# A local-attention kernel on one Trainium2 core: AV with V as the stationary operand, and the softmax divided ahead of the transposes

## The chip, the core and the metric

The kernel runs on one core of a Trainium2 chip (trn2). A core has five engines that run side by side: TensorE (PE in the profile; its weight loads are a row of their own, PEld), VectorE (DVE), ScalarE (ACT), GpSimd (POOL) and SyncE (SP), which here only issues DMAs. The metric is the device time of one execution in microseconds (us); lower is better. A "record" below is one line of the hardware trace: a matmul of fp32 data leaves two pairs of records, each a weight load (the stationary operand) and a matmul (the moving operand streamed through it), and an fp32 transpose leaves one pair.

## The reference

The model is a linear recurrence (8 sequences of 512 steps, width 128) and then six layers of local attention and feed-forward on its output. The change touches the attention alone. Cut to that:

```python
DIM = 128; DEPTH = 6; HEADS = 16; DIM_HEAD = 64; WINDOW = 32; QK_SCALE = 8.0
def local_attention(q, k, v):
    b, h, n, d = q.shape                  # 8, 16, 512, 64
    w = WINDOW; nw = n // w
    bq = q.reshape(b, h, nw, w, d)
    ...
    bk2, bv2 = (look(bk), look(bv))       # each block with the one before it: 64 keys
    ...
    sim = jnp.einsum('bhwie,bhwje->bhwij', bq, bk2) * QK_SCALE
    sim = jnp.where(mask, -jnp.finfo(sim.dtype).max, sim)
    attn = jax.nn.softmax(sim, -1)
    out = jnp.einsum('bhwij,bhwje->bhwie', attn, bv2)
    return out.reshape(b, h, n, d)

def attn_layer(x, Wqkv, qs, ksc, Wo):
    ...
    out = local_attention(q, k, v)
    out = out.transpose(0, 2, 1, 3).reshape(b, n, INNER)
    return out @ Wo
```

All of it is fp32.

## The kernel before

**Tiling.** One *group* is one sequence with half of its heads: 8 heads, held as 4 pairs (`GP = 4`). There are 6 layers x 8 sequences x 2 halves = 96 groups (in layer 0, whose input comes out of the recurrence a quarter at a time, a group is a 128-position chunk of four sequences instead; the work is of the same size). A group has 512 positions, worked through in four *slots* of 128 (`t = 0..3`), and a slot has four blocks of 32 queries (`BT = 4`, `QB = 32`), each of which sees 64 keys (`KB = 64`). There are thus 96 x 4 = 384 slots.

**The attention of one slot.** `scores(t)` does 32 small matmuls (4 pairs x 4 blocks x 2 heads of the pair) into a PSUM area `sc` that ScalarE has filled with the mask before (`mask`). `less_max` takes the maximum of each row and subtracts it (two VectorE instructions, from PSUM into the SBUF tile `e`), and `exps` does the exponential on ScalarE in place. One slot later, `turn` transposes the exponentials, four transposes of 128 x 128 into the PSUM tile `tp`, and ScalarE copies them to `eT`. `average` is the product with V, the AV of the title: 32 matmuls, each with 32 columns of `eT` as the stationary operand (64 keys x 32 queries) and 65 columns of V as the moving one, of which the last is a column of ones, so that the sum of the exponentials comes out as a 65th column. The two heads of a pair lie in partitions 0 to 63 and 64 to 127 (`rows`), and the four query blocks go to the four 32-partition strips of the output. The output of each head goes into a PSUM bank of its own (`av`, two of them), queries on the partitions. `divide` (VectorE) inverts the 65th column and multiplies, twice, into `ao`. One slot later again `turn_back` transposes `ao` with four more transposes, so that the head dimension is on the partitions, and ScalarE copies that to `aoT`. `project` multiplies with `Wo` (4 matmuls of 512 columns), once in a group, and `add` adds it to the residual.

**Order.** Nothing reorders the work: the order on every engine is written out by hand in `mixed` and `dense`, which lay one slot's attention of the group `cur` between the projections of the groups behind it in line: `one` (its norms `sums`, its values `values`, its rotary finish) and `two` (`unit_a`, `unit_b`: the query and key projections, 512 columns each), while `old` is the group before (its `project`). `last` is the slot one earlier, `back` the slot two earlier. Each engine works through its own queue in order and waits on semaphores.

**Stages.** While the recurrence still runs (groups up to `NREC = 9`), `mixed` is used: after each piece of TensorE work `rec.tick(us)` issues the next step of the recurrence if at least `PACE = 0.35` us of work have been laid in between. Steps that find no place run `alone`, beside matmuls that only keep TensorE busy (`warm`, L361). After that `dense` is used for the remaining 87 groups, with the feed-forward (`Feed`) laid in after every eight groups.

**Buffers.** The PSUM pool `acc` has two banks, which `tp`, the two `av`, `at` and the feed-forward's output take in turn. `mm` has four banks in the dense stage (three before), and `sc` has two. `e`, `eT` and `ao` have one buffer each, `aoT` one for a whole group. V lies in `vbufs`, 65 wide a head (`VW = DH + 1`), written by `values`, with SBUF-to-SBUF DMAs (`between`) that copy each block next to its neighbour.

Of the kernel before, what the change touches and what calls it, by code (L numbers as in the profile page):

```python
# [27 lines left out]
GP = 4  # L28
# [7 lines left out]
VW = DH + 1  # L36
# [12 lines left out]
def mk_seq_preln_kernel(  # L49
# [44 lines left out]
    for i in range(2):  # L94
        vb = const.tile([P, NBLK, GP, VW], F32, name=f"vbuf{i}")
        nc.gpsimd.memset(vb, 0.0)
        nc.gpsimd.memset(vb[:, :, :, DH:], 1.0)
        vbufs.append(vb)
# [53 lines left out]
    with tc.tile_pool(name="qk", bufs=2) as qkp, tc.tile_pool(  # L152
# [323 lines left out]
        class Group:  # L476
# [172 lines left out]
            def exps(self):  # L649
                nc.scalar.activation(self.e, self.e, AF.Exp, scale=QK_SCALE)  # L650

            def turn(self, t):
                nm = f"{self.nm}_{t}"
                tp = accp.tile([P, GP, P], F32, tag="acc", name=f"tp_{nm}")
                for i in range(GP):
                    nc.tensor.transpose(  # L656
                        tp[:, i, :], self.e[:, i].rearrange("p a k -> p (a k)"), ident
                    )
                rec.tick(0.5)
                self.eT = ep.tile([P, GP, P], F32, tag="eT", name=f"eT_{nm}")  # L660
                nc.scalar.copy(self.eT, tp)  # L661

            def average(self, t):
                self.avs = [
                    accp.tile(
                        [P, GP, P], F32, tag="acc", name=f"av_{self.nm}_{t}_{par}"
                    )
                    for par in range(2)
                ]
                for i in range(GP):  # L670
                    for blk in range(BT):
                        for par, av in enumerate(self.avs):
                            rows = slice(par * KB, (par + 1) * KB)
                            nc.tensor.matmul(  # L674
                                av[blk * QB : (blk + 1) * QB, i, :VW],
                                self.eT[rows, i, blk * QB : (blk + 1) * QB],
                                self.v[rows, BT * t + blk, i, :],
                                start=True,
                                stop=True,
                                skip_group_check=True,  # L680
                            )
                rec.tick(0.8)

            def divide(self, t):
                nm = f"{self.nm}_{t}"
                self.ao[t] = ep.tile(
                    [P, GP, 2, DH], F32, tag="ao", name=f"ao_{nm}", bufs=1
                )
                for par, av in enumerate(self.avs):
                    rc = small.tile([P, GP], F32, tag="rc", name=f"rc_{nm}_{par}")  # L690
                    nc.vector.reciprocal(rc, av[:, :, DH])  # L691
                    nc.vector.tensor_mul(  # L692
                        self.ao[t][:, :, par, :],
                        av[:, :, :DH],
                        rc.unsqueeze(2).to_broadcast([P, GP, DH]),
                    )

            def turn_back(self, t):
                if t == 0:
                    self.aoT = aop.tile([P, GP, S], F32, tag="ao", name=f"aoT_{self.nm}")  # L700
                at = accp.tile([P, GP, P], F32, tag="acc", name=f"at_{self.nm}_{t}")
                for i in range(GP):
                    nc.tensor.transpose(  # L703
                        at[:, i, :], self.ao[t][:, i].rearrange("p a d -> p (a d)"), ident
                    )
                rec.tick(0.5)
                nc.scalar.copy(self.aoT[:, :, t * P : (t + 1) * P], at)  # L707
# [258 lines left out]
        def mixed(n, t, cur, one, two, old, last, lt, back, bt):  # L966
# [10 lines left out]
            if old and t == 1:  # L977
                fill[3] = [lambda: old.project(wo)]
# [22 lines left out]
            if back:  # L1001
                back.turn_back(bt)
# [10 lines left out]
            if one and t == 1:  # L1013
                one.finish(1)
            if last:
# [5 lines left out]
            if last:  # L1021
                last.divide(lt)
# [4 lines left out]
        def dense(t, cur, one, two, old, last, lt, back, bt, feed):  # L1027

            def softmax():
                if cur:  # L1030
                    cur.less_max(t)
                    cur.exps()
                    if t + 1 < NT:
                        cur.mask(t + 1)
                    elif one:
                        one.mask(0)

            if last:
                last.turn(lt)
            if back:  # L1040
                back.turn_back(bt)
# [3 lines left out]
            if cur:  # L1045
                cur.scores(t)
            if t == 0:
                softmax()
# [13 lines left out]
                if last:  # L1062
                    last.average(lt)
                    last.divide(lt)
# [3 lines left out]
            if t == 1:  # L1068
                softmax()
                if old:  # L1070
                    old.project(wo, (0, 1))
                if one:
                    one.finish(1)
                if last:
                    last.average(lt)
                    last.divide(lt)
                if old:
                    old.project(wo, (2, 3))
                    old.add()
                if one:  # L1080
                    one.finish(2)
# [7 lines left out]
            if t >= 2:  # L1089
                if two and not (feed and t == 2):  # L1090
                    two.unit_b(u)
                softmax()
                if last:
# [3 lines left out]
                    last.divide(lt)  # L1097
# [14 lines left out]
        def slot(n, t, feed=None):  # L1112
# [10 lines left out]
            back, bt = (cur, t - 2) if t > 1 else (old, NT - 2 + t)  # L1123
            if n < NREC:
                mixed(n, t, cur, one, two, old, last, lt, back, bt)
            else:
                dense(t, cur, one, two, old, last, lt, back, bt, feed)
# [185 lines left out]
```

## Time and profile before

| What | us |
|---|---|
| Median of 3 runs | 3746.9 (3741.02 to 3747.28) |
| Profiled execution, device time | 3752.48 |
| Its span (first to last instruction) | 3750.3 |
| DVE busy, share of the span | 2585.7 (69%) |
| ACT busy | 1929.7 (51%) |
| POOL busy | 1826.5 (49%) |
| POOL, L548 and L549, the two largest groups of any engine | 766.3 and 756.8 |
| ACT, the copies `eT` (L661) and `aoT` (L707), 320 each | 190.1 and 193.7 |
| DVE, `ao` (L692), 640 | 271.8 |
| `warm` matmuls of the steps that run alone (L361), 182 steps | 69.7 + 49.9 |
| Mean granted TensorE clock | 0.977 of full speed |

The span is read in two parts: up to about 597 us the recurrence runs (512 steps, the last tanh at 596.5 us), and from there on the dense order repeats. The row maxima (L640, one for each slot) show its period: outside the feed-forward, four slots of a group take 28.5 to 31 us, and every eighth group, with a feed-forward between, some 70 us.

### The profile page before, as it was taken

What the parts mean: (1) busy time and instruction counts of PE and PEld (TensorE: products, weight loads), DVE (VectorE), ACT (ScalarE), POOL (GpSimd) and SP (SyncE); (2) the same over time, 40 slices, a digit from 0 to 9 for tenths busy, and PEclk for the clock granted to TensorE, in tenths of its full rate; (3) what the DMA queues carried; (4) which work ended last, traced back from release to release, by engine and by line L of the source; (5) the groups of instructions that cost most, each with busy time, mean ns of one, the idle gap of its engine ahead of it and who ended that gap; (6) DMA issues with size and microseconds to landing.
All of it is one profiled execution on the core that took longest, in us unless ns stands there. A gap on an engine that the chain in (4) does not pass through costs nothing.

```text
span 3750.3 us, 158910 instructions
## 1 busy us (share of the span) xinstructions
PE 3546.2 (95%) x70180; PEld 2137.0 (57%) x70180; DVE 2585.7 (69%) x5200; ACT 1929.7 (51%) x3864; POOL 1826.5 (49%) x780
## 2 busy tenths in 40 slices
PE   8889987999999999999999999999999999999997
PEld 4556664555566556556565565555556565565553
DVE  3455565767677677677677677677677677677673
ACT  2344443545565455455466455455455465465552
POOL 1442332636366366366366366466466465465450
PEclk9988988999999999999999999999999999999998
DMA  4233433554355345345245355355355255355242
GB/s 128 53 93 78 101 84 75 127 117 108 86 117 119 70 113 132 81 105 124 67 114 138 76 115 113 73 130 124 80 115 116 68 130 124 74 115 120 67 111 56
DMA packets 355866, 378.20 MB, mean 101 GB/s; under 512 B 93550, under 2 KB 254572, under 8 KB 355052
## 3 DMA queue, kind: packets, MB, share of 16 engines
q1 hardware_dynamic: 354172, 365.78, 42.7%
q8 instruction: 554, 9.08, 1.1%
q10 hardware_dynamic: 1008, 2.27, 0.2%
q14 instruction: 132, 1.08, 0.1%
HBM read 34.56 MB, written 14.20 MB: 13 GB/s over the span
## 4 chain that ended last, share of the span: by engine, by line
PE 80%; DVE 11%; ACT 4%; issue 3%; DMA 1%; SPq 1%; DVEq 0%; ACTq 0%
PE yo L713 8%; PE rawb L538 8%; PE rawa L526 8%; PE sc L627 8%; PE av L674 5%; PE tp L656 5%; PE nsq L430 4%; PE at L703 4%; PE yf L912 3%; PE xb L281 3%; PE fa L886 3%; PE fg L890 3%; PE vps L587 3%; PE bc L465 2%; PE warm L361 2%
## 5 line engine op out<-in xcount | busy, mean ns | idle before, releaser
L548 POOL TENSOR_TENSOR u<-rope_sb,bs 128x1024 f32<-128x1024 f32 x320 | 766.3, 2395 | 1228.8 <-ACT bs L544 1066.4
L549 POOL TENSOR_TENSOR t<-t,u 128x1024 f32<-128x1024 f32 x320 | 756.8, 2365 | 25.1
L516 DVE SCALAR_TENSOR_TENSOR t<-rawa,par_sb,rope_sb 128x1024 f32<-128x1024 f32 x320 | 410.5, 1283 | 214.9 <-ACT sq L530 200.7
L650 ACT ACTIVATE e<-e 128x512 f32<-128x512 f32 x320 | 201.7, 630 | 371.5 <-DVE e L643 229.6
L565 DVE TENSOR_TENSOR t<-t,bc 128x1024 f32<-128x1024 f32 x320 | 381.9, 1214 | 14.7 <-PE bc L465 10.2
L661 ACT COPY eT<-tp 128x512 f32<-128x512 f32 x320 | 190.1, 594 | 349.1 <-PE tp L656 348.6
L674 PEld LDWEIGHTS av<-vbuf,eT 64*32 64x32 f32 x20480 | 228.0, 105 | 215.0 <-issue 139.1
L526 PE MATMUL rawa<-xbuf,wqk 128*128 128x512 f32 x640 | 342.8, 617 | 0.0
L538 PE MATMUL rawb<-xbuf,wqk 128*128 128x512 f32 x640 | 342.4, 617 | 0.0
L587 PE MATMUL vps<-wv,xbuf 128*64 128x256 f32 x2560 | 315.8, 387 | 8.3 <-DVE xf L864 8.3
L713 PE MATMUL yo<-aoT,wo 128*128 128x512 f32 x640 | 319.5, 622 | 0.9 <-ACT aoT L707 0.9
L627 PEld LDWEIGHTS sc<-kbuf,qT 64*32 64x32 f32 x20480 | 227.2, 105 | 144.8 <-ACT sq L542 57.0
L674 PE MATMUL av<-vbuf,eT 64*32 64x65 f32 x20480 | 283.4, 225 | 6.4 <-issue 5.3
L692 DVE TENSOR_TENSOR ao<-av,rc 128x256 f32<-128x256 f32 x640 | 271.8, 425 | 22.0
L627 PE MATMUL sc<-kbuf,qT 64*32 64x64 f32 x20480 | 282.1, 225 | 1.7 <-issue 1.5
L640 DVE TENSOR_REDUCE mx<-sc 128x8 f32<-128x512 f32 x320 | 219.6, 686 | 91.9 <-PE sc L627 91.7
L281 PEld LDWEIGHTS xb<-hT,s1w 128*128 128x128 f32 x1022 | 168.9, 197 | 172.9 <-ACT hT L289 118.5
L596 ACT COPY vbuf<-vps 128x512 f32<-128x512 f32 x320 | 188.2, 588 | 141.2 <-PE vps L587 138.4
L542 ACT ACTIVATE sq<-rawb 128x512 f32<-128x512 f32 x320 | 189.7, 593 | 129.6 <-PE rawb L538 129.1
L587 PEld LDWEIGHTS vps<-wv,xbuf 128*64 128x64 f32 x2560 | 168.4, 136 | 151.1 <-DVE rc L691 48.5
L289 ACT ACTIVATE hT<-xb 128x8 f32<-128x8 f32 x512 | 91.5, 179 | 291.8 <-PE xb L281 276.5
L643 DVE TENSOR_TENSOR e<-sc,mx 128x512 f32<-128x512 f32 x320 | 221.3, 692 | 11.0
(282 smaller groups left out, 6280.1 us busy)
## 6 DMA issues: line engine op xcount, KB each, us to landing
qT<-t SPq DMA_DIRECT2D x640, 128.0 KB
kbuf<-t SPq DMA_DIRECT2D x640, 128.0 KB
vbuf<-vbuf SPq DMA_DIRECT2D x544, 130.0 KB
vbuf<-vbuf SPq DMA_DIRECT2D x160, 97.5 KB
wqk<-in_w_qkv SPq DMA_DIRECT2D x12, 512.0 KB
xbuf<-xT SPq DMA_DIRECT2D x48, 128.0 KB
xf<-xT SPq DMA_DIRECT2D x24, 256.0 KB
xf<-xT SPq DMA_DIRECT2D x24, 255.5 KB
```

The lines of the kernel that those rows point to most:

```text
L281: nc.tensor.matmul(self.xb[:, k, :], abc[:, 0, :], self.hT[:, (t - 1) % P, :], start=False, stop=True, skip_group_check=True,)
L516: nc.vector.scalar_tensor_tensor(t, self.twice(raw), scale, self.rope(isk, 1), ALU.mult, ALU.mult)
L526: nc.tensor.matmul(raw, self.wqk[:, c, 0], self.xs[:, WINDOW:], start=True, stop=True)
L538: nc.tensor.matmul(raw, self.wqk[:, c, 1], self.xs[:, WINDOW:], start=True, stop=True)
L548: nc.gpsimd.tensor_mul(self.wide(u), self.rope(isk, 0), self.twice(bs))
L549: nc.gpsimd.tensor_add(self.ts[c], self.ts[c], u)
L565: nc.vector.tensor_mul(t, t, self.bcs[c].unsqueeze(1).to_broadcast([P, 2, S]))
L587: nc.tensor.matmul(ps[par * KB : (par + 1) * KB, j], self.xs[:, k0 : k0 + KB], self.wv[:, par * GP * DH : (par + 1) * GP * DH], start=True ...
L627: nc.tensor.matmul(self.sc[blk * QB : (blk + 1) * QB, par, i, :], self.qT[rows, i, q0 : q0 + QB], kT[rows, i, :], start=False, stop=True, ...
L674: nc.tensor.matmul(av[blk * QB : (blk + 1) * QB, i, :VW], self.eT[rows, i, blk * QB : (blk + 1) * QB], self.v[rows, BT * t + blk, i, :], s ...
L692: nc.vector.tensor_mul(self.ao[t][:, :, par, :], av[:, :, :DH], rc.unsqueeze(2).to_broadcast([P, GP, DH]),)
L713: nc.tensor.matmul(self.yp, wo[:, self.g * GP + c, :], self.aoT[:, c, :], start=(c == 0), stop=(c == GP - 1),)
```

## The change

- V becomes the stationary operand of AV (64 keys x 64 head columns) and 32 columns of `eT` the moving one. The output then has the head dimension on the partitions, both heads of a pair in one PSUM bank, and ScalarE copies it straight to `aoT`. `turn_back`, its transposes and the tile `ao` are gone.
- Since the sum over the keys can no longer ride along as a 65th column, the exponentials are summed and divided ahead of `turn`: `exps` now writes a PSUM tile `ex` out of the pool `acc`, and `divide` sums it over the keys, inverts the sums and multiplies into the SBUF tile `p`, which `turn` transposes.
- V is 64 wide (`VW = DH`), and the column of ones is gone with its memset.
- The order: `aoT` is ready a slot earlier (`last` in place of `back`). In `dense`, `scores` now comes first in a slot, `turn` second, and `unit_a` after `less_max`; at `t = 1`, the whole of `project` stands ahead of `average` instead of half of it on each side. In `mixed`, `project` stands between the mask and `average`.

```diff
-VW = DH + 1
+VW = DH
...
-        nc.gpsimd.memset(vb[:, :, :, DH:], 1.0)
...
             def exps(self):
-                nc.scalar.activation(self.e, self.e, AF.Exp, scale=QK_SCALE)
+                self.ex = accp.tile(
+                    [P, GP, 2, KB], F32, tag="acc", name=f"ex_{self.nm}"
+                )
+                nc.scalar.activation(self.ex, self.e, AF.Exp, scale=QK_SCALE)
+
+            def divide(self, t):
+                nm = f"{self.nm}_{t}"
+                rc = small.tile([P, GP, 2], F32, tag="rc", name=f"rc_{nm}")
+                nc.vector.reduce_sum(rc, self.ex, AX.X)
+                nc.vector.reciprocal(rc, rc)
+                self.p = ep.tile([P, GP, 2, KB], F32, tag="p", name=f"p_{nm}")
+                nc.vector.tensor_mul(
+                    self.p, self.ex, rc.unsqueeze(3).to_broadcast([P, GP, 2, KB])
+                )
 
             def turn(self, t):
...
-                        tp[:, i, :], self.e[:, i].rearrange("p a k -> p (a k)"), ident
+                        tp[:, i, :], self.p[:, i].rearrange("p a k -> p (a k)"), ident
...
             def average(self, t):
-                self.avs = [
-                    accp.tile(
-                        [P, GP, P], F32, tag="acc", name=f"av_{self.nm}_{t}_{par}"
-                    )
-                    for par in range(2)
-                ]
+                nm = f"{self.nm}_{t}"
+                if t == 0:
+                    self.aoT = aop.tile([P, GP, S], F32, tag="ao", name=f"aoT_{nm}")
+                av = accp.tile([P, GP, P], F32, tag="acc", name=f"av_{nm}")
                 for i in range(GP):
                     for blk in range(BT):
-                        for par, av in enumerate(self.avs):
+                        for par in range(2):
                             rows = slice(par * KB, (par + 1) * KB)
                             nc.tensor.matmul(
-                                av[blk * QB : (blk + 1) * QB, i, :VW],
+                                av[rows, i, blk * QB : (blk + 1) * QB],
+                                self.v[rows, BT * t + blk, i, :],
                                 self.eT[rows, i, blk * QB : (blk + 1) * QB],
-                                self.v[rows, BT * t + blk, i, :],
...
                 rec.tick(0.8)
-
-            def divide(self, t):
...
-                for par, av in enumerate(self.avs):
-                    rc = small.tile([P, GP], F32, tag="rc", name=f"rc_{nm}_{par}")
-                    nc.vector.reciprocal(rc, av[:, :, DH])
-                    nc.vector.tensor_mul(
...
-            def turn_back(self, t):
...
-                for i in range(GP):
-                    nc.tensor.transpose(
-                        at[:, i, :], self.ao[t][:, i].rearrange("p a d -> p (a d)"), ident
-                    )
-                rec.tick(0.5)
-                nc.scalar.copy(self.aoT[:, :, t * P : (t + 1) * P], at)
+                nc.scalar.copy(self.aoT[:, :, t * P : (t + 1) * P], av)
```

The order in `dense`, for the slots `t >= 2`, is now `scores`, `turn`, `less_max`, `unit_a`, `exps` with the next mask, `unit_b`, `average`, `divide`, `unit_a`, `unit_b`; before it was `turn`, `turn_back`, `unit_a`, `scores`, `unit_b`, `less_max` with `exps` and the mask, `average`, `divide`, `unit_a`, `unit_b`.

## The prediction, made before the change was run

> **What bounds the kernel now.** I read three views in this order: the page's sums and its chain of waits over the whole span, the sums of the dense stage alone, and then the chain of waits inside one slot, because a share of the span says nothing of what one slot's work is worth.
>
> ```profile
> PE 3546.2 (95%) x70180; PEld 2137.0 (57%) x70180; DVE 2585.7 (69%) x5200; ACT 1929.7 (51%) x3864; POOL 1826.5 (49%) x780
> PE 80%; DVE 11%; ACT 4%; issue 3%; DMA 1%; SPq 1%; DVEq 0%; ACTq 0%
> 862.00:3648.00 2786.00, 2715.17 (x57623) 1611.21 (x57616) 2051.05 (x3910) 1546.44 (x2791) 1518.07 (x643) 1.00 0.46 105
> ```
>
> The third line is the dense stage: span, then busy time of PE, PEld, DVE, ACT and POOL, and the granted clock. TensorE is busy 97% of it at full clock, VectorE 74%, ScalarE 56%. So TensorE sets the time there, and an instruction on it costs the time until the next can begin. That is what the chain inside one slot (t = 2 of a group) shows; columns are start, duration, what, records:
>
> ```profile
> 2009.00 0.44 PE tp L656 x4
> 2009.43 0.44 PE at L703 x4
> 2009.87 0.86 PE rawa L526 x2
> 2010.73 0.79 PE sc L627 x53
> 2011.52 1.05 PE rawb L538 x2
> 2012.58 0.79 PE av L674 x53
> 2013.37 1.05 PE rawa L526 x2
> 2014.42 0.87 PE rawb L538 x2
> 2015.30 0.64 PE tp L656 x4
> ```
>
> Only PE stands in it. AV takes 0.79 us of a slot, the transposes back 0.44. A full-width matmul that follows tiled ones takes 1.05 rather than 0.86: a change of tiling costs some 0.19.
>
> **The weight load.** Swapping the operands leaves the number of matmuls alone, but each weight load now has 64 columns instead of 32, and each streams 32 columns instead of 65. So the price of a load by its width decides. Timeline of the weight loads, cut at chosen places (start, length from first start to last end):
>
> ```profile
> 2004.29 0.30 PEld L713 LDWEIGHTS yo<-aoT,wo 128*128 128x128 f32 x2 [0.16 <-ACT aoT L707]
> 1997.54 0.14 PEld L587 LDWEIGHTS vps<-wv,xbuf 128*64 128x64 f32 x2 [0.20 <-issue]
> 1997.54 0.20 PEld L587 LDWEIGHTS vps<-wv,xbuf 128*64 128x64 f32 x4 [0.20 <-issue]
> 2001.29 1.01 PEld L465 LDWEIGHTS bc<-k,selt_sb 32*128 32x128 f32 x32 [0.31 <-ACT vbuf L596]
> 2001.32 1.17 PE L465 MATMUL bc<-k,selt_sb 32*128 32x128 f32 x32 [0.18 <-DVE k L456]
> 2012.51 0.70 PEld L674 LDWEIGHTS av<-vbuf,eT 64*32 64x32 f32 x64 [0.76 <-issue]
> ```
>
> A record of a load includes latency, so its length (0.19 us at 128 columns) isn't its price; the distance to the next load into the same tile of the array is. At 128 columns: 0.30 for two, less 0.19, is 0.11 (0.108 in the records' starts). At 64 columns: the first two loads fill two column tiles, the next two go to the same tiles and end 0.20 - 0.14 = 0.06 later (starts 1997.536 and 1997.591, 55 ns). At 32 columns, in AV, the first two into one tile start at 2000.276 and 2000.305, 29 ns. So a load takes some 0.85 ns a column. Loads into different tiles overlap: 64 AV loads in 0.70 us, though 64 x 29 ns is 1.86; 32 `bc` loads in 1.01 us, though 32 x 0.108 is 3.5. And loads are hidden by the matmul before them in the same tile: `bc` does 8 loads and 8 matmuls of 128 columns in each of four row tiles in 1.17 us, where 8 x (0.108 + 0.109) would be 1.7 (0.109 is the pitch of the transposes, also 128 columns). In `bc` both overlap at a pitch of 0.112.
>
> The old AV used 8 tiles (two halves of the rows, four query strips), so each loaded 8 times. In the new one, head `par` has rows `par*64...` and output partitions `par*64...`: two tiles only, on the diagonal, and each takes 32 of the 64 records.
>
> **The change, part by part**, per slot:
>
> 1. AV. Each tile takes 32 loads of 55 ns. A matmul of 32 columns streams in 27 ns (0.109 / 4) and hides behind the next load. Pitch 55 to 59 (the 4 ns that `bc` shows over its load); I take 56: 32 x 56 = 1.79 us, plus about 0.13 until the next instruction (before: 0.79 less the 0.65 to the last start, a little less for the shorter matmul) = 1.92. Before 0.79: **+1.13** (bounds +1.08 and +1.24).
> 2. `turn_back`: 4 x 0.109 = **-0.44**.
> 3. Changes of tiling. Counted along the new order, a group has 18 rather than 20, since at t = 1 `project` is no longer cut by AV: -2 x 0.15 = **-0.3 a group** (bounds 0.15 and 0.36).
> 4. VectorE. Off: two reciprocals and two multiplications. On: a sum of 128x512 from PSUM (as the maximum, L640), one reciprocal, one multiplication of 128x512 from PSUM (as L643).
>
> ```profile
> L640 DVE TENSOR_REDUCE mx<-sc 128x8 f32<-128x512 f32 x320 | 219.6, 686 | 91.9 <-PE sc L627 91.7
> L643 DVE TENSOR_TENSOR e<-sc,mx 128x512 f32<-128x512 f32 x320 | 221.3, 692 | 11.0
> L691 DVE RECIPROCAL rc<-av 128x4 f32<-128x4 f32 x640 | 112.1, 175 | 42.0 <-PE av L674 30.8
> L692 DVE TENSOR_TENSOR ao<-av,rc 128x256 f32<-128x256 f32 x640 | 271.8, 425 | 22.0
> ```
>
> 1.55 on against 2 x (0.175 + 0.425) = 1.20 off: +0.35 a slot, 134 us in all, costed at nothing because VectorE stays near 75% of a longer slot. What it could cost is that `turn` now waits for `divide` rather than for the exponential alone. At t = 2 the way from the end of `scores` to `p` is 0.2 + 0.69 + 0.69 + 1.28 (L516, which stands in VectorE's queue ahead of `divide`, and covers the exponential) + 1.55 = 4.4 us; behind `divide` wait only the next L516 and then the rotary finishes. TensorE meanwhile has `turn`, four projections, AV and the next `scores`: 0.44 + 3.8 + 1.9 + 0.8 = 6.9. At t = 1: 4.4 (with the 1.21 of L565) against 0.4 + 3.4 + 1.9 + 0.8 = 6.5. At t = 0 the nine steps of `solve` stand ahead of `divide`, about 8.2 against 10. Two microseconds are left everywhere; each 0.1 us beyond them would cost 38 us.
> 5. ScalarE and DMAs: the exponential writes PSUM instead of SBUF (0.58 for L617, which writes PSUM, to 0.69 for L544; before 0.63), and `aoT` is a copy of the same shape. Zero, and hidden in an engine at 56%. Banks of `acc`: one tile less a slot, each taken after a copy that the order needs anyway. DMAs: same number, rows 1.5% shorter; nothing waits for them in the chain shown.
> 6. The recurrence. Without the tick of `turn_back` the mixed stage lays in fewer steps. Counted in the built order, 212 steps run alone instead of 182. A lone step takes 0.655 us (23 of them from 581.9 to 596.4), one laid in 0.22 (median to the next piece of work): 30 x 0.435 = **+13**.
> 7. TensorE's small waits for `bc` (12.5 us, behind VectorE's `solve`) vanish under the longer AV: **-13**.
>
> A rule of the Trainium skill speaks for a still worse outcome ("TensorE: Matmul & The Clock Gate", Part 3, The mechanism): a weight load overlaps a matmul in flight only if they are in different row groups. By it each load would wait for its own tile's matmul, and the estimate would be the time of the second rival below. The `bc` rows disagree with it, and I go by them.
>
> **Sum.** 36 mixed slots: 36 x 0.69 + 13 = 38. 87 dense groups: 87 x (4 x 0.69 - 0.3) = 214. Less 13: +239, onto 3752.5 of the profiled execution: 3991. The median of the runs lies 5.6 lower: 3986, rounded to **3988 us**. By the bounds of 1, 3, 6 and 7: +200 to +310, that is 3945 to 4060.
>
> **The rivals.**
>
> *Weight loads don't bound AV (faster).* If loads into the diagonal tiles came twice as fast, or two could be held in waiting, streaming would bound it: 32 x 27 ns + 0.13 = 0.99 us, +0.20 a slot. With the transposes gone and fewer changes of tiling that is -0.24 x 384 - 26 = -118: about 3630. It decides below a pitch of 36 ns, where AV is 1.29 and the parts cancel. For it: AV has never run with two tiles of 64 x 64 here. Against: three widths lie on one line, at the first load into a tile, where nothing else could hold it up. 8%.
>
> *Loads are not hidden.* Pitch 55 + 27 = 82, AV 2.75, another 0.83 x 384 = 320: about 4310. Against it `bc`. 7%.
>
> *`p` comes late.* If VectorE's chain takes over 2 us longer than figured, TensorE waits at `turn`; 0.3 us a slot would give 4100. For it: VectorE has 11% of the chain already. 5%.
>
> **How the numbers follow.** The forecast has 80%. The range 3900 to 4085 takes its bounds, and half of the third rival. Chances: faster 8%, slower 91%, within 0.2% (7.5 us, about what a measurement of this kernel can tell) 1%, since only a pitch right at 36 ns would give it.
>
> **What would show it.** Right: AV at some 1.9 us to the next instruction, its 64 loads spread over some 1.8 us and PEld nearly idle-free there; no `at`; the dense group some 2.5 us longer than its 28.5 to 31; waits of `tp` for `p` near zero; 212 lone steps. Wrong: AV near 1 us (the first rival) or 2.7 (the second), or a large wait of PE at `turn` for VectorE's multiplication.

## The result, and the profile after

| | before | after |
|---|---|---|
| Median of 5 runs each, us | 3741.02 (3736.80 to 3747.28) | 3928.56 (3923.21 to 3932.14) |
| Ratio to before, 95% interval | 1 | 1.0494 [1.0476, 1.0512] |
| Span of the profiled execution, us | 3750.3 | 3926.7 |
| Mean granted TensorE clock | 0.977 | 0.977 |

The change made the kernel 187.5 us slower by the medians, 176.4 by the spans (the profiled execution before took 3752.48 us, some 11 above its median). The forecast was 3988, that is +241 onto the median of 3746.9 known then: its sign and the cost that it put on AV's weight loads were right, and the loss was about a quarter smaller than worked out.

Busy times and the chain of waits over the whole span of the changed kernel:

```profile
PE 3771.7 (96%) x68702; PEld 2452.8 (62%) x68704; DVE 2743.8 (70%) x4816; ACT 1988.1 (51%) x3864; POOL 1820.3 (46%) x778
PE 93%; DVE 3%; issue 2%; ACT 1%; DMA 1%; POOL 0%; SPq 0%; POOLq 0%; ACTq 0%; DVEq 0%
```

Its sums over the same window of the dense stage as in the prediction (span, then busy PE, PEld, DVE, ACT and POOL, and the granted clock):

```profile
862.00:3648.00 2786.00, 2763.48 (x53216) 1783.00 (x53217) 2079.61 (x3423) 1525.60 (x2659) 1433.89 (x608) 1.00 0.44 99
```

TensorE now carries 93% of the chain instead of 80%, and VectorE 3% instead of 11%: in the dense stage TensorE is busy 99% of the time. The chain inside slot t = 2 of one group (start, duration, what, records) can be laid beside the one in the prediction:

```profile
2017.80 0.79 PE sc L626 x53
2018.59 0.59 PE tp L668 x4
2019.17 0.86 PE rawa L525 x2
2020.04 0.86 PE rawb L537 x2
2020.89 1.99 PE av L684 x64
2022.88 1.05 PE rawa L525 x2
2023.93 0.86 PE rawb L537 x2
2024.79 0.79 PE sc L626 x53
```

AV went from 0.79 to 1.99 us and `at` is gone. The other steps differ only by what now stands ahead of them, which moves a change of tiling of 0.15 to 0.2 us. The weight loads of that group's AV and of the `bc` after it (timeline of PEld: start, time from first start to last end) show why:

```profile
2007.59 1.95 PEld L684 LDWEIGHTS av<-eT,vbuf 64*64 64x64 f32 x64 [0.38 <-ACT vbuf L595]
2009.58 0.98 PEld L464 LDWEIGHTS bc<-k,selt_sb 32*128 32x128 f32 x32
```

64 loads into two tiles take 1.95 us. The last load's own length is 0.135, so the 31 steps of 32 in each tile have a pitch of (1.95 - 0.135) / 31 = 59 ns.

Who is late, summed over most of the dense stage (TensorE's list of waits from 900 to 3640 us: line that waited, releaser, us in total, times, longest); first the kernel before, then the changed one:

```profile
PE nsq L430 <- issue: 22.5, 29, 1.5
PE bc L465 <- DVE k L456: 12.5, 63, 0.2
...
PE tp L656 <- ACT e L650: 5.0, 10, 0.5
```

```profile
PE vps L586 <- DVE xf L850: 8.2, 10, 0.8
PE av L684 <- ACT eT L673: 7.3, 10, 0.7
PE fa L872 <- ACT gl L884: 4.0, 10, 0.4
PE tp L668 <- issue: 1.5, 1, 1.5
```

Before, TensorE stood 66.3 us in that window (the whole list; three of its lines are shown); after, 21.0. The two largest waits before, `nsq` and `bc`, are gone. The wait of `nsq` has no releaser that the profile shows. In the timeline of PE it lies inside `nsq`, behind the 64 matmuls of `sc`:

```profile
1993.67 0.87 PE L627 MATMUL sc<-kbuf,qT 64*32 64x64 f32 x64
1994.47 0.64 PE L430 MATMUL nsq<-sq,sel_sb 128*32 128x128 f32 x14
1995.89 1.72 PE L430 MATMUL nsq<-sq,sel_sb 128*32 128x128 f32 x50 [0.78 <-issue]
```

Whether the longer AV or the new order closed these two waits is taken up below.

**Where the time went.** The table takes TensorE's time from the first start of one kind of work (its first weight load) to the first start of the next, as means over the plain groups (no feed-forward) from the 20th on. It was computed from the records; the last three columns belong to versions explained further down.

```
us a plain group      before   after   own bank,    beside the   values
                                       bc in acc    scores       early
AV                      3.48    7.95      4.26         4.26       4.27
at                      2.11    0         0            0          0
rawa + rawb             8.15    7.68      7.89         8.50       7.83
nsq                     2.31    1.88      1.90         1.98       2.08
bc                      1.13    1.10      1.80         1.47       1.44
sc                      3.33    3.20      3.32         3.28       3.33
yo                      3.31    3.63      3.63         3.63       3.63
tp                      1.98    2.03      1.85         1.77       1.78
vps                     3.75    3.75      3.95         3.76       3.81
sum                    29.55   31.22     28.60        28.65      28.17
```

By the row maxima, which mark the groups, the 73 plain groups from the 12th on went from 29.60 to 31.10 us, and the 11 intervals that hold a feed-forward from 70.01 to 71.65. The nine mixed groups took 49 us more in all. Over the 87 dense groups that is 127 us, and 127 + 49 = 176 is the difference of the spans. The table's sums lie 1.67 us apart where the row maxima give 1.50, so its parts hold to some 0.2 us a group. A wait stands in the row of the work ahead of it: AV's 3.48 before holds TensorE's wait for `bc` at t = 0, where the next matmul came 1.03 us after AV's first one on average (900 to 3640 us) instead of 0.79.

### The profile page after: what moved, and what is told of

Same layout as the page of the kernel before. It is cut to its first block, busy times and chain, and to the rows that moved or that the text cites. A ratio compares the mean times of both kernels' runs of the same rounds, so it can differ in the third digit from the quotient of the medians.

```text
span 3926.7 us, 154971 instructions
## 1 busy us (share of the span) xinstructions
PE 3771.7 (96%) x68702; PEld 2452.8 (62%) x68704; DVE 2743.8 (70%) x4816; ACT 1988.1 (51%) x3864; POOL 1820.3 (46%) x778
## 4 chain that ended last, share of the span: by engine, by line
PE 93%; DVE 3%; issue 2%; ACT 1%; DMA 1%; POOL 0%; SPq 0%; POOLq 0%; ACTq 0%; DVEq 0%
PE av L684 16%; PE rawa L525 8%; PE sc L626 8%; PE vps L586 8%; PE yo L699 7%; PE rawb L537 7%; PE tp L668 5%; PE nsq L429 4%; PE xb L280 3%; PE yf L898 3%; PE fa L872 3%; PE fg L876 3%; PE bc L464 2%; PE warm L360 2%; PE cp L819 1%
## 5 line engine op out<-in xcount | busy, mean ns | idle before, releaser
L684 PEld LDWEIGHTS av<-eT,vbuf 64*64 64x64 f32 x20480 | 623.7, 135 | 220.8 <-ACT sq L529 110.7
L684 PE MATMUL av<-eT,vbuf 64*64 64x32 f32 x20480 | 659.1, 220 | 11.7 <-ACT eT L673 11.7
L693 ACT COPY aoT<-av 128x512 f32<-128x512 f32 x320 | 187.6, 586 | 398.3 <-PE av L684 398.3
L537 PE MATMUL rawb<-xbuf,wqk 128*128 128x512 f32 x640 | 326.8, 592 | 0.0
L699 PE MATMUL yo<-aoT,wo 128*128 128x512 f32 x640 | 297.4, 608 | 1.2 <-ACT aoT L693 0.7
L529 ACT ACTIVATE sq<-rawa 128x512 f32<-128x512 f32 x320 | 191.7, 599 | 123.9 <-PE rawa L525 123.9
L660 DVE TENSOR_TENSOR p<-ex,rc 128x512 f32<-128x512 f32 x320 | 221.3, 692 | 28.2 <-PE av L684 1.4
L652 ACT ACTIVATE ex<-e 128x512 f32<-128x512 f32 x320 | 191.8, 599 | 94.8 <-DVE e L642 94.5
```

The source lines that it names most:

```text
L537: nc.tensor.matmul(raw, self.wqk[:, c, 1], self.xs[:, WINDOW:], start=True, stop=True)
L660: nc.vector.tensor_mul(self.p, self.ex, rc.unsqueeze(3).to_broadcast([P, GP, 2, KB]))
L684: nc.tensor.matmul(av[rows, i, blk * QB : (blk + 1) * QB], self.v[rows, BT * t + blk, i, :], self.eT[rows, i, blk * QB : (blk + 1) * QB], ...
L699: nc.tensor.matmul(self.yp, wo[:, self.g * GP + c, :], self.aoT[:, c, :], start=(c == 0), stop=(c == GP - 1),)
```

## The experiments

Each ratio is to runs of the kernel before on the same chip.

### Do weight loads bound AV?

Each matmul of AV streams 64 columns instead of 32, and so writes 64:

```diff
-                                av[rows, i, blk * QB : (blk + 1) * QB],
+                                av[rows, i, blk // 2 * KB : (blk // 2 + 1) * KB],
...
-                                self.eT[rows, i, blk * QB : (blk + 1) * QB],
+                                self.eT[rows, i, blk // 2 * KB : (blk // 2 + 1) * KB],
```

> The changed kernel, but each matmul of AV streams 64 columns of eT instead of 32 (its block's queries and the neighbour block's; the later block overwrites the earlier one's columns, so half of AV's result is the neighbour's). Theory, AV is set by its weight loads, one of 64 columns each 58 ns into each of two tiles: streaming 64 columns takes 54 ns and stays hidden, AV stays at 1.99 to 2.05 us a slot, the time within 15 us of the 3928 of the changed kernel. Rival A, streaming sets it: the pitch doubles, AV 3.8 us, about 4630. Rival B, a load of about 30 ns followed by a stream of 27, not overlapped: pitch 85, AV 2.85, about 4260.

Measured: 3933.52 us, ratio 1.0500 [1.0483, 1.0517]: the changed kernel's own 1.0494. The chain inside one slot of this version has

```profile
2018.09 2.01 PE av L684 x64
2020.11 0.79 PE sc L626 x53
```

against 1.99. Twice the streaming costs 0.02 us a slot, so the stream lies wholly behind the loads. That also settles the second rival: if a load waited for the matmul in its own tile, 27 ns more of streaming would have added 32 x 27 = 0.86 us. The rule of the Trainium skill that the prediction set aside ("TensorE: Matmul & The Clock Gate", Part 3, The mechanism), that a load overlaps a matmul in flight only in another row group, does not hold for these tiles.

The counterpart cuts each load in two of 32 columns, so that four tiles share them, at twice the number of instructions:

```diff
-                        for par in range(2):
...
+                        for h in range(2):
+                            for par in range(2):
...
+                                    av[d0 : d0 + QB, i, blk * QB : (blk + 1) * QB],
+                                    self.v[rows, BT * t + blk, i, h * QB : (h + 1) * QB],
```

> The changed kernel, but each load of V is split into two of 32 columns (two strips of the output), so AV has twice the loads and matmuls, in four tiles of 64 x 32. Theory, a load costs by its columns: 32 records a tile at 30 ns, 0.96 + 0.13 = 1.1 us, or 1.45 if the engine can't issue faster than the 128 loads and matmuls in 0.65 us of the kernel before; less 0.54 to 0.89 a slot, 3590 to 3720. Rival, a fixed price of each load and matmul in its tile, whatever its width: 32 x 58 ns as now, about 3930. Rival, a fixed price in each half of the rows: AV 3.8 us, about 4630.

Measured: 4057.86 us, ratio 1.0826 [1.0798, 1.0854]. AV itself did get shorter where nothing broke it, but elsewhere TensorE stood (timeline of PE: start, first start to last end, in brackets the idle time before and its releaser):

```profile
2003.72 0.92 PE L626 MATMUL sc<-kbuf,qT 64*32 64x64 f32 x50
2007.24 0.46 PE L626 MATMUL sc<-kbuf,qT 64*32 64x64 f32 x12 [2.60 <-issue]
...
2011.12 1.29 PE L686 MATMUL av<-eT,vbuf 64*32 64x32 f32 x128
2012.34 1.13 PE L525 MATMUL rawa<-xbuf,wqk 128*128 128x512 f32 x2
```

Its list of waits from 900 to 3640 us:

```profile
PE sc L626 <- issue: 122.9, 90, 2.8
PE av L686 <- issue: 32.3, 52, 2.0
```

128 pairs in 1.29 us is about 5 ns a record, and behind such a burst the next 64 pairs break off for up to 2.8 us with nothing to wait for that the profile shows. The granted clock fell too: from 862 to 3640 us it was 0.97 here and 1.00 in the changed kernel, and in the 3.7 us after the hole shown (2007.3 to 2011.0) it was 0.62, so that this hole cost more than its length. The time that was expected was missed. AV alone does answer the question on the load's width: each of its four tiles takes 32 loads, as each of the two in the changed kernel, and at half the width AV takes 1.22 us to the next matmul (2011.12 to 2012.34) instead of 1.99. A fixed price of each load, whatever its width, falls by that. The run also shows that the number of small matmuls in a row has a price of its own; that the supply of instructions sets it is the likely reason, but it was not tested.

### What were the transposes and the waits worth?

The changed kernel, and the kernel before, each with the four transposes of `turn` issued twice:

```diff
-                for i in range(GP):
+                for i in (*range(GP), *range(GP)):
```

> The changed kernel with the four transposes of turn done twice in each slot (the second time over the first), as the price of the four transposes that the change removed. Theory, TensorE sets the time everywhere and nothing is absorbed: 4 x 0.109 x 384 = +167, about 4095. Rival, part of such an addition falls into waits: under +120.

> The kernel before with the four transposes of turn done twice in each slot. Theory, added TensorE work is partly absorbed in the kernel before, whose TensorE idles 86 us of the dense stage in small waits (30 of them without a releaser) against 35 in the changed kernel: clearly less than the +137 that the same addition cost the changed kernel, +80 to +115. Rival, no difference between the two: +130 to +145.

Measured: 4065.19 us, ratio 1.0858 [1.0835, 1.0881], and 3850.01 us, ratio 1.0262 [1.0246, 1.0277]. The same 4 x 384 transposes cost 0.0364 of the time before (136 us) in the changed kernel and 0.0262 (98 us) in the one before. By 4 x 0.109 us a slot it would be 167 in both; the changed kernel's 136 lies between its theory and its rival, and why it isn't 167 was not followed up. In the kernel before, part of the added work fell into time in which TensorE stood: its `nsq` fell from 2.35 to 1.93 us a group, 87 x 0.42 = 37 us, about the whole difference of the two, and in its list of waits `nsq <- issue` fell from 22.5 to 0.3 us. So the kernel before takes in some 0.4 us a group of transposes added ahead of `sc` for nothing. That other added work would fare the same was not tried.

The new order of `dense` alone, in the kernel before:

```diff
+            if cur:
+                cur.scores(t)
             if last:
                 last.turn(lt)
...
-                cur.scores(t)
...
-                    old.project(wo, (0, 1))
+                    old.project(wo)
```

> The kernel before (old operands, transposes back, division after AV) with only the new order of the dense stage: scores first, turn and turn_back next, unit_a after less_max, project whole ahead of AV. Theory, of the 0.6 us a group by which the changed kernel came out better than the sum, the larger part is its order (18 changes of tiling instead of 20): -0.3 to -0.5 us in 87 groups, -26 to -45, about 3700 to 3720. Rival, the long AV covered small waits and the order alone does nothing: 3741 to 3748 as before; or it is worse, because turn_back now stands ahead of the projections.

Measured: 3801.81 us, ratio 1.0136 [1.0117, 1.0154]: slower, not faster. Without the change's AV the order has waits of its own, as TensorE's list from 900 to 3640 us says:

```profile
PE yo L713 <- ACT aoT L707: 58.9, 76, 1.1
PE sc L627 <- ACT sc L617: 20.0, 63, 0.6
```

`turn_back` of the last slot stands right ahead of `project` in this order, so the copy to `aoT` isn't covered. The order only fits a kernel without `turn_back`, and this run doesn't tell what the fewer changes of tiling were worth.

It does tell the two vanished waits apart. `bc <- DVE k` is still in its list, with 13.3 us, so the order alone doesn't close that one. `nsq <- issue` isn't in it: from the first matmul of `nsq` to the next work it takes 1.89 us on average, against 1.88 in the changed kernel and 2.32 in the kernel before (900 to 3640 us). This order lays the transposes between the 64 small pairs of `sc` and the 64 of `nsq`. A version below (with a PSUM bank of its own for the exponentials) needs 1.07 us a slot for AV, where AV and the transposes back took 0.79 + 0.44 before, and has only 53.4 us of waits in its list; it has no `nsq <- issue` either:

```profile
2005.28 0.87 PE L629 MATMUL sc<-kbuf,qT 64*32 64x64 f32 x64
2006.09 0.65 PE L673 MATMUL tp<-ident,p 128*128 128x128 f32 x4
2006.67 1.96 PE L432 MATMUL nsq<-sq,sel_sb 128*32 128x128 f32 x64
```

So the order closes this hole, and the longer AV isn't needed for it. That the transposes in between give the supply of instructions its time is argued, not shown.

### Can the loads be shared by four tiles?

64 columns of V fit any of four 64 x 64 tiles. The changed kernel uses the two on the diagonal. Here the odd pairs swap their two heads' output halves (and `Wo` its rows to match), so that odd pairs use the other diagonal, and the loop over the pairs moves inside that over the blocks, so that the four tiles take turns. Each diagonal writes a bank of `acc` of its own, so AV takes two, and the exponentials stay in SBUF:

```diff
-                self.ex = accp.tile(
...
+                self.ex = self.e
...
+                            to = (par + i) % 2 * DH
...
-                                av[rows, i, blk * QB : (blk + 1) * QB],
+                                avs[i % 2][to : to + DH, i // 2, blk * QB : (blk + 1) * QB],
```

> The changed kernel, but the odd pairs of heads write their two halves to the other partitions (the rows of Wo are swapped to fit), so that AV's 64 x 64 loads go into four tiles in turn instead of two on the diagonal; two PSUM banks for AV, and the exponentials stay in SBUF so that the banks suffice. Number and shape of the matmuls are the same. Theory, loads into one tile follow each other at 58 ns and tiles load side by side: 16 loads a tile, 16 x 0.058 + 0.13 = 1.06 us, less 0.93 a slot, 384 slots: -356, about 3575, or up to 3640 if small waits come back that the long AV had covered. Rival, loads of one half of the rows (or all loads) share a path: AV stays near 2.0, about 3930.

Measured: 3805.08 us, ratio 1.0158 [1.0139, 1.0176]. AV fell to 1.065 us a slot, as the theory has it: 16 loads a tile instead of 32. But of 87 x 3.67 = 319 us only 0.0336 of the time before, 126 us, came out. TensorE's list of waits from 900 to 3640 us comes to 165.8 us, against 21.0 in the changed kernel, and most of it is

```profile
PE tp L669 <- DVE p L661: 101.4, 72, 2.1
```

VectorE's group of that multiplication (busy in all, mean ns of one), and then the timeline of all engines around it, cut to the two lines and a later one:

```profile
L661 DVE TENSOR_TENSOR p<-e,rc 128x512 f32<-128x512 f32 x320 | 475.9, 1487 | 28.2 <-PE rawa L528 0.9 <-DVE rc L659 0.5
```

```profile
2003.97 2.42 POOL L550 TENSOR_TENSOR u<-rope_sb,bs 128x1024 f32<-128x1024 f32 x1
...
2004.10 2.84 DVE L661 TENSOR_TENSOR p<-e,rc 128x512 f32<-128x512 f32 x1
...
2011.47 0.69 DVE L661 TENSOR_TENSOR p<-e,rc 128x512 f32<-128x512 f32 x1
```

With both operands in SBUF the multiplication takes 0.69 us when GpSimd is idle (at 2011.47), and when it starts just behind a GpSimd instruction it ends 0.55 us after that one's end (2004.10 + 2.84 = 2006.94; GpSimd's ends at 2006.39). So it waits until that instruction is done. In the whole trace 190 of its 384 executions start while a GpSimd instruction runs, and 189 of these end 0.5 to 0.6 us after it; where the multiplication starts first, or GpSimd is idle, it takes 0.69. This agrees with the Trainium skill ("SBUF — State Buffer", Who interferes with whom): a VectorE operation with two SBUF inputs contends with a GpSimd operation that reads SBUF, and the port pair that they share is an exclusive lock. With `ex` in PSUM, as the change has it, the mean is 692 ns. So the PSUM tile of the change isn't a detail.

The next four versions look for a PSUM bank for `ex`; edits are shown against the version that each builds on, cut to what matters. First one of the four banks of `mm`, with `divide` ahead of `solve` at t = 0:

```diff
-                self.ex = self.e
+                self.ex = mm(f"ex_{self.nm}").rearrange(
+                    "p (i a k) -> p i a k", a=2, k=KB
+                )
```

> The kernel with four tiles for AV, with the exponentials in a PSUM bank of the pool mm instead of SBUF (division ahead of solve at t = 0, and ahead of the feed-forward's scale, so that the banks suffice). Theory, what the four tiles gained was lost at VectorE's multiplication p <- e, rc, 1487 ns on average with both operands in SBUF against 692 with one in PSUM, and at the waits for it (107 us of TensorE for p, 27 for t): with PSUM 692 again, waits for p near zero, 3805 - 134 = about 3670, and down to 3575 if all of the AV gain (0.93 x 384) remains. Rival, the multiplication is slow in this order for another reason, or the two AV banks cost elsewhere: 3780 to 3805.

Measured: 4055.19 us, ratio 1.0809 [1.0793, 1.0825]. That is above both ranges. The multiplication is back at 692 ns, but two other waits have grown (TensorE's list of waits, whole span):

```profile
PE yo L707 <- DVE t L567: 177.4, 73, 2.5
PE bc L467 <- DVE k L458: 90.3, 70, 1.6
```

`yo` comes out of `mm` and waits for VectorE's rotary finish (`t`), which reads the banks of `mm` that hold the norms: the missing bank fits that, but it wasn't tried apart from the new order. `bc` waits for `k`, the result of `solve`, which stands behind `divide` in this version.

Then a bank of its own in the dense stage, three left for `mm`, the norms' `spread` cut in three quarters and one:

```diff
-                    mmp = mms.enter_context(tc.tile_pool(name="mm", bufs=4, space=PSUM))
+                    mmp = mms.enter_context(tc.tile_pool(name="mm", bufs=3, space=PSUM))
+                    exps_bank.append(
+                        mms.enter_context(tc.tile_pool(name="exb", bufs=1, space=PSUM))
+                    )
...
-                    one.spread(range(4))
+                    one.spread((0, 1, 2))
...
+                    one.spread((3,))
```

> Four tiles for AV, and in the dense stage the exponentials in a PSUM bank of their own, taken from mm (three banks instead of four). So that three suffice, AV stands ahead of the last values at t = 0, the fourth bc is spread at t = 1 after project, the feed-forward's scale is spread in two halves, and its gates go to acc. Theory, AV at 1.06 us is worth 3.7 us a group, VectorE's multiplication stays at 692 ns, and what the kernel with four tiles and the one with the bank from mm lost were waits for p and for mm banks: a group of 31.2 - 3.7 + 0.4 (one more change of tiling) = 27.9 us against 29.3 in the kernel before, in 87 groups -120, about 3600 to 3660, faster than both. Rival, with fewer TensorE microseconds another chain ends last (VectorE at 75% and in order): waits of TensorE over 200 us, 3720 or more.

Measured: 3810.95 us, ratio 1.0150 [1.0133, 1.0167]. TensorE hardly waits (53.4 us from 900 to 3640), yet nothing is gained on the version in SBUF. The timeline of PE shows what was paid:

```profile
2012.51 0.49 PE L467 MATMUL bc<-k,selt_sb 32*128 32x128 f32 x4
2013.26 1.15 PE L467 MATMUL bc<-k,selt_sb 32*128 32x128 f32 x20 [0.27 <-ACT vbuf L598]
2019.98 1.15 PE L467 MATMUL bc<-k,selt_sb 32*128 32x128 f32 x8
```

One row tile alone needs as long for its 8 records (1.15 us) as four tiles side by side for their 32 in the kernel before (1.17): the fourth quarter by itself costs a second 1.15 us, and the first three start 0.75 us late behind ScalarE's copy out of the bank used last. So the sums of the fourth quarter were put into a bank of `acc`, beside the three others:

```diff
-                bcs = {c: mm(f"bc_{nm}_{c}") for c in cs}
+                bcs = {c: mm(f"bc_{nm}_{c}") for c in cs[:3]}
+                if len(cs) == 4:
+                    bcs[cs[3]] = accp.tile(
...
```

> The kernel with an own bank for the exponentials (3810.95 us, before 3753.65 beside it), with the one thing its trace blames undone: its norms were spread for three quarters of a group and then for the fourth alone, and that cost 3.34 us of TensorE a group against 1.27 in the kernel before. Here the fourth quarter's sums go into a bank of AV's pool, so that the spread is again one run of 16 steps over four row tiles; in exchange finish of the fourth quarter stands ahead of AV at t=1 and those of the second and third behind it. Theory (AV on four tiles at 1.07 us a slot is what it costs, and nothing else of the rearrangement binds): 87 dense groups x 2.0 = 174 us off, to 3600 to 3680, a ratio of 0.96 to 0.98 to before, the first version faster than before; bc back to 1.3 us a group. Rival (the bank is only passed on: AV at t=1 or the projection now waits for VectorE's finishes, or TensorE's sequencer is as full): 3740 to 3830, with TensorE's idle time ahead of av or yo rising from 74 us to over 150.

Measured: 3744.48 us, ratio 0.9993 [0.9984, 1.0002], no change against before: the loss is gone, but the expected 3600 to 3680 was missed. `bc` fell from 2.88 to 1.80 us a plain group (by the table's rule) and not by 2.0, for the late start was left, as the timeline of PE shows:

```profile
2010.12 0.49 PE L471 MATMUL bc<-k,selt_sb 32*128 32x128 f32 x4
2010.87 1.16 PE L471 MATMUL bc<-k,selt_sb 32*128 32x128 f32 x28 [0.27 <-ACT vbuf L602]
```

To avoid that, two quarters in `mm` and two in `acc`, and `project` cut in two around `turn`:

```diff
-                self.bcs.update(self.inv.spread(cs, nm))
+                self.bcs.update(self.inv.spread(cs, nm, 2 if len(cs) == 4 else 3))
...
+            if old and t == 1:
+                old.project(wo, (0, 1))
             if last:
                 last.turn(lt)
```

> The kernel before it (3744.48 us, ratio 0.9993 to before) still starts its spread of the norms 0.75 us late in every group: after four matmuls it stands until ScalarE has copied the last values out of the bank that the third quarter's sums need (idle 0.27 us, and the next matmul starts 0.75 us after the first). Here two quarters go to the values' pool and two to AV's, so that no bank of the four was written last; finish of the two quarters in AV's pool stands first, and the projection is cut in two halves around the turn of t=1, which covers the first finish. Theory (that start is all that is left over): bc from 2.25 to 1.3 us a group, 87 dense groups x 0.8 = 70 us off, to 3660 to 3700, a ratio of 0.975 to 0.988, faster than before. Rival (the finishes ahead of less_max make the exponentials or the turn late, and TensorE waits there instead): 3720 to 3780, with TensorE waiting for t L569, p or e in its list of waits by over 40 us.

Measured: 3769.88 us, ratio 1.0082 [1.0068, 1.0096], slower again. `bc` did come to 1.11 us a plain group, but `scores` now stood 33.1 us with the releaser "issue" (22 times, up to 2.4 us), in the slot after the cut projection; the rival had named other waits. That it is the supply of instructions again, since only four long matmuls now stand ahead of 64 + 64 small pairs instead of eight, fits the narrow loads above but was not tried by itself.

The last two leave order and pools as the change has them. The scores fill half of each of their two banks, and the exponentials go into the other halves:

```diff
-                self.ex = self.e
+                self.ex = exs
...
+        exs = sct[:, :, GP * KB :].rearrange("p a (i k) -> p i a k", k=KB)
```

> Four tiles for AV as in the second kernel (3805.08 us, where the multiply that divides took 1487 ns on two SBUF operands and TensorE waited 107 us for it), but without a PSUM bank taken from anything: the scores fill half of each of their two banks, and the exponentials go into the other halves. The order, the four banks of values and norms and the two of AV stay as in the changed kernel. Theory (AV's loads are all that the change costs, and the earlier versions lost it again through SBUF and through the missing bank): the multiply at about 700 ns, no wait for p, AV 4.3 us a group instead of 7.94: 96 groups x 3.6 = 350 us off 3928 at the most, less some of what the small waits that AV covered cost: 3590 to 3680, a ratio of 0.96 to 0.985, faster than before. Rival (VectorE reads a bank that TensorE and ScalarE write at the same time, and is slowed as it was by SBUF; or the supply of small matmuls binds): 3740 to 3810 again, with TensorE's waits for p or 'issue' over 80 us.

Measured: 3697.74 us, ratio 0.9888 [0.9870, 0.9906]: 1.1% faster than the kernel before, though 18 us above the range. The multiplication takes 692 ns, so the shared bank doesn't slow it. It makes TensorE wait instead, in its list from 900 to 3640 us:

```profile
PE sc L630 <- DVE p L662: 72.4, 133, 3.2
```

and, in order of time, in the chain of waits of one slot t = 2 (start, duration, what):

```profile
2001.30 1.13 DVE t L568
2002.43 0.60 DVE xT L717
2003.03 1.13 DVE t L568
2004.16 0.61 DVE mx L643
...
2007.81 0.70 DVE p L662
2008.51 0.14 issue
2008.64 0.85 PE sc L630 x50
```

The next `scores` write the banks that `divide` still reads, and so stand until it is done; it is late there because two rotary finishes and the residual of t = 1 stand ahead of the maximum in VectorE's queue. At t = 3 TensorE has the last block of values to do and no wait. So that block moves one slot up:

```diff
-                if one and t == 3 and not feed:
+                if one and t == 2 and not feed:
                     one.values(3)
                     one.between(1)
```

> The version with the exponentials beside the scores (3697.74 us, ratio 0.9888) waits at one place: at t=2 of a plain group the next scores stand 0.74 to 0.82 us until VectorE has read the exponentials in the same bank (72 us in the list of waits, all but 20 of them there), while at t=3 TensorE has a block of values to do (1.01 us) and no wait. Here that block, with its two DMAs, moves from the end of t=3 to the end of t=2. Theory (TensorE does it in the time in which it stood, and VectorE is done at t=3 without it): 64 to 68 groups x 0.8 = 51 to 54 us off, to 3635 to 3660 by this call's before of about 3740, a ratio of 0.972 to 0.98. Rival (the wait only moves to t=3 or to t=0, where the last VectorE step then comes late): 3685 to 3710, with TensorE still waiting over 50 us for p.

Measured: 3664.23 us against 3751.46, ratio 0.9769 [0.9752, 0.9787]. TensorE's wait for `p` in the same window:

```profile
PE sc L630 <- DVE p L662: 23.8, 66, 2.2
```

48.6 us of the wait are gone and 0.0119 of the time before, some 45 us. This version is 2.3% faster than the kernel before. It has the change's order but for that block, and V as the stationary operand of AV.

## Why the prediction was right, and where its sizes were off

- **AV, +1.13 a slot.** Right in its mechanism, and a little low: AV takes 1.99 us to the next instruction where 1.92 was foreseen, +1.20 a slot, between the 1.13 and the upper bound of 1.24. The pitch is 59 ns (55 to 59 foreseen, 56 taken), and the version that streams twice as much shows that loads set it. The table's +4.47 a plain group lies near 4 x 1.13 = 4.52 by luck: 4 x 1.20 is 4.80, and the row before held some 0.24 us of the wait for `bc`. The first rival (streaming bound) and the second (loads not hidden) fall by the run that streams twice as much.
- **`turn_back` and the changes of tiling, 4 x -0.44 - 0.3 = -2.06 a group.** Right within 0.15: `at` -2.11, `rawa` and `rawb` -0.47, `yo` +0.32, `tp` +0.05: -2.21.
- **VectorE at nothing.** Right. The reduction took 682 ns, the reciprocal 203, the multiplication 692, which is 1.58 against 1.55 foreseen, and `turn` waited 0.8 us for `p` in the whole run. The third rival falls. What the slack was worth shows where it is taken away: with the multiplication at 1487 ns, 101 us of waits.
- **The recurrence.** 212 lone steps, as counted from the order. But the nine mixed groups took 49 us more instead of 38. The lone steps end at 643.8 us instead of 596.4, so nearly all of it lies ahead of the recurrence's end; which piece of the mixed order takes the other 11 was not tried.
- **The small waits, -13, and the new order, -0.3 a group: the terms that were too small.** The prediction took `bc`'s 12.5 us as covered by the longer AV, and that holds: with the new order alone it stays at 13.3 us, with the change it is gone. The line above it in the same list, `nsq <- issue` with 22.5 us, was left out. It vanished too: `nsq` fell by 0.43 us a plain group, `sc` by 0.13 and `bc` by 0.03, together 0.59, or 51 us over 87 groups. For `nsq` that was the order's doing, since the order alone brings it from 2.32 to 1.89 us. The prediction counted the order by its changes of tiling and did not ask what it does to the holes of a path that it took to be set by TensorE alone.

By the groups: foreseen 214 - 13 = 201 us dense and 38 mixed; measured some 127 and 49. A plain group was to grow by 2.31 us (201 over 87) and grew by 1.67 in the table: AV with `bc`'s wait +0.10 against the sum, `turn_back` and tiling -0.15, `nsq`, `sc` and `bc` -0.59. By the row maxima it grew by 1.50, and the last 0.2 us stay open.

The forecast of 3988 stands two above the 3986 that the prediction's own sum gives. The measured 3928.56 lies below 3945, the least that its bounds add up to; it is inside the stated range only because that began at 3900, for which no term is given. In that the range was lucky.

## What to carry to other kernels

Swapping the operands of small matmuls trades streaming for weight loads: count the loads that each tile of the array takes, times the pitch for their width, before counting the transposes saved; here 32 x 59 ns in each of two tiles decided it, and four tiles instead of two, once a place for the exponentials was found and one block of values was moved, turned +4.9% into -2.3%. When work is added to a saturated engine or its order is changed, first ask which small waits that will close, those with no named releaser too, and try the order alone. A bank or an operand moved to make room is a change in itself: look for the engine that shares it.

## What the runs showed of the hardware that was not expected

- A long run of small matmuls can be followed by a hole that no other engine explains: 128 pairs go out in 1.29 us, but the matmuls behind them then break off for up to 2.8 us; 123 us ahead of `scores` in that version, whose granted clock in the dense stage was 0.97 instead of 1.00.
- Loads into different 64 x 64 tiles run side by side: AV's 64 loads and matmuls need 1.99 us in two tiles, in four 1.07.
- Four row tiles of `bc` side by side need 1.17 us for their 32 records, one alone 1.15 us for its 8.
- A VectorE multiplication of 128x512 with both operands in SBUF took 0.69 to 2.87 us beside GpSimd, mean 1487 ns; with one operand in PSUM it took 690 to 693 ns every time.
